# Two input loads, a pair of first maxima and the last batches' small work at other places in a cross-attention kernel

## The chip, the core and the metric

The kernel runs on one core of a Trainium2 chip. The core has five engines with queues of their own: TensorE (PE in the profile; its weight loads are listed apart as PEld), VectorE (DVE), ScalarE (ACT), GpSimd (POOL) and SyncE (SP). Each engine works through its queue in order, and SP does nothing here but issue DMA transfers. POOL issues a few transfers too, on a DMA queue of its own. The metric is device time in microseconds of one execution, the median over several runs; lower is better. Beside it there is one profiled execution, from which all rows of the profile come.

## The reference

Eight batches of 112 queries with 320 channels attend to 375 context rows of 512 channels. The last four context rows are image prompts (IP), the other 371 are text. There are 20 heads of 16 channels. In short:

```python
q   = heads(x @ W_q);  k_t = heads(text @ W_k);  v_t = heads(text @ W_v)
probs_t  = softmax(q k_t^T / 4)                     # 112 x 371 for each batch and head
text_out = probs_t @ v_t
qsem  = l2norm(probs_t @ text)                      # 112 x 512 for each head
sem   = qsem @ l2norm(ip)^T                         # 112 x 4
fused = q k_ip^T / 4 + 0.5 * sem
ip_out = (softmax(fused) * mask) @ v_ip
out = (text_out + ip_out) @ W_out + b_out + x
```

The kernel does not form `qsem`. It multiplies the probabilities by a matrix with the context's Gram matrix, the products with the prompts and the head's values side by side; the norm follows from the Gram part by a product with the probabilities and a sum, `ss`.

## The kernel before

The work of a batch is cut into five groups of four heads, so there are 40 steps (b, g). For one step:

- TensorE makes four scores, one for each head (`scores`, L648).
- VectorE takes the first maxima of their rows, negated (`probabilities`, L661, tile `nmx`). ScalarE does the exps with them (L665, tile `p`) and for later batches copies the four prompt logits (L667, `ipl`).
- SP copies the four probabilities into another arrangement (L672, `xg` from `p`; `xg` is one of a ring of two tiles), and VectorE transposes 32x32 blocks of it (`transposed`, L684, `xgT`). A step's transposes can be done in two halves.
- TensorE does the products with `u`, the Gram matrix and the values: 12 blocks of rows of four heads each (`product`, L696, into `ps_qd`).
- VectorE multiplies the Gram part with the probabilities and sums (`reduced`, L749), and ScalarE copies the value part (`value_sums`, L723, tile `pvs`). For the last batch some heads go another way: `shared(b, g, n)` gives n of a group's four heads to ScalarE (copies L733 and L734, sums L742) and POOL (products L738), and `reduced` does the rest.
- POOL puts the values into `u` for the next steps (`placed`, L614).

`finish(b)` is what remains for a batch: a generator that yields between its pieces. It normalises, does the small softmax over the prompts, multiplies with the prompts' values on POOL (L831, L834), adds both halves to the attention `ah` (L838, L839), transposes it on TensorE (L844, `ps_a`), projects it (L853, `ps_o`), adds input and bias (L859, `ob`) and writes it out. `run(key, make, pieces)` advances a generator by that many pieces. The last batch (b = 7) has `ending` in place of it; in its case the input and the bias are added by `with_bias(b)` (L763) on POOL. `x_sb` holds the inputs; `load_inputs(b0, b1)` (L308) loads those of some batches with one transfer of POOL's queue.

The order on each engine is written by hand: the scope is `manual_schedule`, and instructions stand in each queue in the order of the program. After a start, `alone(0)` does the products of the first step. From then on `pair(n)` does two steps, n and n + 1, in one stream of products, with the scores, maxima and exps of the steps two ahead placed among the products, and `behind(n)` does what lies between pairs: keys, values, queries and Gram matrices of the next batches, and pieces of `finish`. `steps` has its index n from 0, so pair(1) is (0,1) and (0,2), pair(3) is (0,3) and (0,4), pair(5) is (1,0) and (1,1), pair(7) is (1,2) and (1,3). A loop over the last batch's groups closes the program, with the pieces of batch 6's `finish` (key `before`) between its steps.

In `pair(n)`, `coming_scores` and `coming_probabilities` are called for the heads (2, 3) at j = 0 and for (0, 1) at j = 1, and the second half of the next step's transposes follows at j = 1. The first half is done by the `tr(1)` of the `behind` before. The transfers of SP use eight semaphores in turn, so that a transfer waits until the one eight before it has landed.

Of the kernel before, what the change touches and what calls it, by code (L numbers as in the profile page):

```python
# [20 lines left out]
def kernel(  # L21
# [588 lines left out]
    def placed(b, g, chunks=range(NT)):  # L610

        s = st[b]
        for c in chunks:
            nc.gpsimd.tensor_copy(  # L614
                region(b, c)[:, :, UV - c * P :], s["vr"][:, c * QN : (c + 1) * QN, g, :]
            )
# [149 lines left out]
    def finish(b):  # L766
# [65 lines left out]
            if some.stop < NIP:  # L832
                yield
        eng.tensor_tensor(wv[:, :2], wv[:, :2], wv[:, 2:], ALU.add)  # L834
        if b == B - 2:
            yield
            eng = nc.vector
        eng.tensor_tensor(ah, ah, wv[:, 0], ALU.add)  # L838
        eng.tensor_tensor(ah, ah, wv[:, 1], ALU.add)  # L839
        yield  # L840

        ps = bank(f"ps_a_{b}", spare=True)
# [246 lines left out]
    def alone(n):  # L1089
# [5 lines left out]
                    coming_probabilities(n + LEAD, heads)  # L1095
        transposed(*steps[n + 1])

    def pair(n):

        one, two = steps[n], steps[n + 1]  # L1100
        b, g = one
        tags = ("mm", "sc") if b % 2 and g == NG - 1 else ("sc", "mm")
        ends = (BLK - 2, BLK - 1)

        products_in(b, g, ("qd",) * GROUP)
        for j in range(BLK - 2):
            product(b, g, j, range(GROUP))
            if j < 2:
                heads = (HIGH, LOW)[j]
                coming_scores(n + LEAD, heads, tags[j])  # L1110
                coming_probabilities(n + LEAD, heads)
            if j == 1:
                transposed(*two, BLK // 2, BLK)
            if j % QN == QN - 1:
                placed(*two, (j // QN,))
        products_in(*two, (tags[1],) * 2 + (tags[0],) * 2)
        for there, here in ((HIGH, LOW), (LOW, HIGH)):
            product(*two, 0, there)
            for j in ends:
                product(b, g, j, here)  # L1120
        del st[b]["xT", g]
        placed(*two, (NT - 1,))
        moved(b, g)
        if g > 1:
            turned(b + 2)
        if b % 2 and g in (0, NG - 1):
            f(b - 1 - (g == 0))
        if g in (1, 2):
            f(b - 1, 3 - g)
        reduced(b, g)  # L1130
        value_sums(b, g)

        b, g = two
        for j in range(1, BLK - 2):
            product(b, g, j, range(GROUP))
            if j == 4:
                coming_scores(n + 1 + LEAD, HIGH, "qd")
                coming_probabilities(n + 1 + LEAD, HIGH)
            if j == 7:
                coming_scores(n + 1 + LEAD, LOW, "qd")  # L1140
                coming_probabilities(n + 1 + LEAD, LOW)
        for heads in (HIGH, LOW):
            for j in ends:
                product(b, g, j, heads)
        del st[b]["xT", g]
        moved(b, g)
        if one in ((b, 2), (b, 3)):
            turned(b + 2, 1 + (one == (0, 3)))
# [17 lines left out]
    def behind(n):  # L1166
# [9 lines left out]
        if b % 2 == 0 and g == 0:  # L1176
# [15 lines left out]
            v(nb)  # L1192
            if n == 0:
                run(("pp",), prompt_projections)
            tr(1)
            if n:
                f(b - 1, 2)
            load_next(b + 2)
            if n == 0:
                load_inputs(1, 3)  # L1200
        elif b % 2 == 0 and g == 2:
            turn[:] = ["qd"] * (6 + (b == 0)) + ["mm"]
            gram_to_groups(nb, (2,))
            if b == 0:
                run(("pp",), None)
            k(nb)
            q(nb, 3)
            tr(0)
            v(nb)
            q(nb)  # L1210
            v(nb)
            if b == 0:
                run(("pp",), None)
            tr(1)
            values_to_dram(nb, nc.sync)
            if b == 0:
                load_channels(nc.gpsimd, wo_sb, w_out)
                nc.gpsimd.dma_start(sm_sb, smask.unsqueeze(1))
                nc.gpsimd.dma_start(bias_sb, b_out.partition_broadcast(S))
            elif b == 2:  # L1220
                load_inputs(5, B)
        elif b % 2 == 0 and nb < B - 1:
            if b == 0:
                load_inputs(3, 5)
            turn[:] = ["qd"] * (4 + (b > 0)) + ["mm", "mm"]
            turned(b + 2)
            q(nb)
            if b > 0:
                f(b - 1)
            else:  # L1230
                run(("t", b), lambda: prompt_logits(b))
            k(nb)
            tr(0)
            if b > 0:
                f(b - 1)
            gr(nb + 1, 3)
            tr(1)
            if b > 0:
                f(b - 1)
            load_next(b + 3)  # L1240
            f(b)
            prompt_values(b)
        elif b % 2 == 0:
            turn[:] = ["qd"] * 4 + ["mm"]
            q(nb, 2)
            f(b - 1)
            k(nb)
            nc.scalar.preload_act_table(AF.Sqrt)
            tr(0)
            f(b - 1, 2)  # L1250
            prompt_values(b)
            f(b, 2)
        elif g == 1:
            turn[:] = ["qd"] * 4 + ["mm"]
            gram_to_groups(nb, (2,))
            q(b)
            k(b)
            nc.scalar.preload_act_table(AF.Sqrt)
            k(nb)
            tr(0)  # L1260
            f(b - 1)
            v(nb)
            tr(1)
            v(nb)
            f(b - 1, 3)
            values_to_dram(nb, nc.sync, 0, 2)
            if b == B - 3:
                prompt_values_by_head()
        else:
            turn[:] = ["qd"] * 3 + ["sc"]  # L1270
            v(nb)
            f(b - 1)
            values_to_dram(nb, nc.sync, 2)
            tr(0)
            k(nb)
            f(b - 1, 2)
            tr(1)
            gram_to_groups(nb, (3,))
            values_to_groups(nb, 2)
# [41 lines left out]
    for g in range(NG):  # L1321
        if g == 1:
            run(("f", b - 2), None)
        for j, _ in enumerate(multiplied(b, g)):
# [7 lines left out]
            if g == 1 and j == BLK // 2:  # L1332
                last_keys(b, ps_qd.tile([P, 512], F32, tag="qd", name=f"ps_k_{b}_{FULL}"))
                run(before, None)
                placed(b, g + 1, (0,))
                with_bias(b)
            if g == 2 and j == 2:
                transposed(b, g + 1)
            if g == 3 and j == 3:
                placed(b, g + 1, (0,))  # L1340
                run(before, None)
                transposed(b, g + 1)
                drain(sums)
        if g == NG - 1:
            break

        n = (3, 3, 2, 1)[g]
        held, sums = sums, shared(b, g, n)
        value_sums(b, g, n)
        next(sums)  # L1350
# [2 lines left out]
        reduced(b, g, n)  # L1353
        placed(b, g + 1, range(g % 2, NT))
        if g > 1:
            run(before, None)
        drain(held)
        next(sums)
    run(before, None)
    drain(sums)  # L1360
    last = ending(b, bd)
    next(last)
    reduced(b, g, 0, 1)
    value_sums(b, g, 1)
    run(before, None)
    next(last)
    value_sums(b, g, 0, 1)
    reduced(b, g, 1)
    next(last)
    run(before, None)  # L1370
    next(last)
    next(last)
    next(last)
    run(before, None, 2)
# [45 lines left out]
```

## Time and profile before

| | us |
|---|---|
| median of 3 runs | 419.34 (417.5 to 419.59) |
| profiled execution | 421.68 |
| its span, first to last instruction | 419.9 |
| mean granted clock of TensorE in it | 0.995 of full speed |
| TensorE busy | 410.9 |
| VectorE busy | 326.9 |
| ScalarE busy | 188.6 |
| POOL busy | 113.2 |

A row of the timeline gives the start and the length in microseconds, the engine, the line, the operation, the tile written and the tile read, and the number of instructions that the row joins; in brackets stands the idle time of that engine before it and what ended it. SPq is the issue of transfers by SP; an issue's length is not the transfer's. A window's row gives, for each engine, busy time and number of instructions, then the granted clock, the share of the 16 DMA engines and the rate.

### The profile page before, as it was taken

The page shows a single profiled execution, that of the slowest core. Times are in us where ns is not written, and L with a number is a line of the kernel's source. Part 1 is how long each engine was busy: PE and PEld are TensorE (multiplying, and loading weights), DVE is VectorE, ACT ScalarE, POOL GpSimd, SP SyncE. Part 2 cuts the span into 40 slices and gives each one's busy share as a digit, 9 for nine tenths or more (in the row PEclk, how much of TensorE's full clock was granted, in tenths as well). Part 3 has the DMA queues.
Part 4 walks back from the last instruction along what each step waited for, and adds up shares of the span by engine and source line. Part 5 has one row for each costly group of instructions (what it writes and reads, how often), then busy time and mean ns, then how long its engine had stood idle before and what let it go on. Part 6 is the DMA issues. An engine that isn't in the chain of part 4 may idle for free.

```text
span 419.9 us, 14045 instructions
## 1 busy us (share of the span) xinstructions
PE 410.9 (98%) x5609; PEld 323.1 (77%) x5609; DVE 326.9 (78%) x694; ACT 188.6 (45%) x655; POOL 113.2 (27%) x265
## 2 busy tenths in 40 slices
PE   8999999989999999999999999999999999999896
PEld 8867788868687877879686877779877878687894
DVE  4256686956889888786889897787888987888985
ACT  3254342333642734423643554333644365346853
POOL 4203130031160244011242136002025126104670
PEclk9999999998999999999999999999999999999999
DMA  8878967686555667676655476567756344666220
GB/s 237 170 187 245 168 157 172 168 213 153 129 145 138 169 144 176 168 171 156 165 139 135 123 171 162 149 165 164 176 143 166 100 120 123 173 151 188 85 65 27
DMA packets 58244, 64.64 MB, mean 154 GB/s; under 512 B 19061, under 2 KB 52041, under 8 KB 58180
## 3 DMA queue, kind: packets, MB, share of 16 engines
q1 hardware_dynamic: 57150, 61.47, 58.3%
q0 software_dynamic: 464, 1.56, 1.7%
q8 instruction: 44, 0.72, 0.8%
q10 hardware_dynamic: 566, 0.72, 0.5%
q14 instruction: 20, 0.16, 0.1%
HBM read 19.03 MB, written 5.22 MB: 58 GB/s over the span
## 4 chain that ended last, share of the span: by engine, by line
PE 91%; SPq 2%; DVE 2%; ACT 1%; POOL 1%; DMA 1%; issue 1%; POOLq 0%
PE ps_qd L696 43%; PE ps_v L533 13%; PE ps_k L494 9%; PE ps_g L468 7%; PE ps_s L648 6%; PE ps_q L339 3%; PE ps_k L511 3%; PE ps_o L853 2%; PE ps_g L438 1%; PE ps_w L425 1%; DMA vr<-vd 1%; SPq L482 1%; SPq L136 1%; PE ps_c L408 1%; PE ps_x L331 0%
## 5 line engine op out<-in xcount | busy, mean ns | idle before, releaser
L696 PE MATMUL ps_qd<-u,xgT 32*112 32x40 f32 (+11 forms) x3840 | 220.0, 354 | 3.4 <-ACT ipl L667 1.8
L696 PEld LDWEIGHTS ps_qd<-u,xgT 32*112 32x112 f32 x3840 | 182.5, 173 | 38.1 <-issue 8.7
L684 DVE STREAM_TRANSPOSE xgT<-xg 128x768 f32<-128x768 f32 (+1 forms) x63 | 123.4, 1977 | 17.3 <-DMA xg<-p 9.5
L665 ACT ACTIVATE p<-ps_s,nmx 112x371 f32<-112x371 f32 x160 | 85.5, 585 | 66.9 <-DVE nmx L661 66.7
L661 DVE TENSOR_REDUCE nmx<-ps_s 112x1 f32<-112x371 f32 x160 | 77.1, 535 | 32.2 <-PE ps_s L648 30.0
L614 POOL COPY u<-vr 128x64 f32<-128x64 f32 x120 | 26.8, 236 | 216.7 <-PE ps_qd L696 133.3
L749 DVE CUSTOM_DVE_ANT_0 p<-ps_qd,p 112x371 f32<-112x371 f32 x151 | 72.8, 538 | 11.4 <-ACT pvs L723 8.3
L648 PE MATMUL ps_s<-kT,qm 32*112 32x375 f32 (+1 forms) x320 | 60.9, 485 | 0.0
L533 PE MATMUL ps_v<-wv_sb,ctxT 128*128 128x320 f32 x192 | 56.1, 439 | 0.3 <-ACT kT L501 0.3
L533 PEld LDWEIGHTS ps_v<-wv_sb,ctxT 128*128 128x128 f32 x192 | 35.3, 190 | 14.7 <-ACT kT L501 1.2
L723 ACT COPY pvs<-ps_qd 112x21 f32<-112x21 f32 x151 | 21.6, 197 | 53.0 <-DVE ss L749 48.2
L494 PE MATMUL ps_k<-ctxT,wk_sb 128*128 128x371 f32 x128 | 43.6, 484 | 0.0
L494 PEld LDWEIGHTS ps_k<-ctxT,wk_sb 128*128 128x128 f32 x128 | 23.0, 190 | 13.2 <-issue 1.3
L468 PE MATMUL ps_g<-ctxT 128*32 128x119 f32 (+11 forms) x672 | 33.0, 343 | 0.0
L468 PEld LDWEIGHTS ps_g<-ctxT 128*32 128x32 f32 x672 | 26.2, 109 | 7.4 <-issue 4.2
L648 PEld LDWEIGHTS ps_s<-kT,qm 32*112 32x112 f32 x320 | 28.0, 171 | 4.8 <-ACT p L665 0.4
L396 DVE STREAM_TRANSPOSE ctxT<-ct 128x512 f32<-128x512 f32 x21 | 22.3, 1072 | 6.9 <-DMA u<-ug 6.9
L540 ACT COPY vext<-ps_v 128x320 f32<-128x320 f32 x24 | 10.2, 425 | 36.3 <-PE ps_v L533 33.9
L667 ACT COPY ipl<-ps_s 112x4 f32<-112x4 f32 x140 | 24.2, 173 | 0.0
L454 ACT ACTIVATE ug<-ps_g 128x375 f32<-128x375 f32 (+2 forms) x24 | 9.1, 377 | 23.3 <-PE ps_g L468 9.0
L455 POOL TENSOR_TENSOR ug<-ug,half 128x128 f32<-128x128 f32 (+1 forms) x24 | 10.6, 451 | 29.2 <-ACT ug L454 29.2
L501 ACT COPY kT<-ps_k 128x371 f32<-128x371 f32 x16 | 7.5, 469 | 22.8 <-PE ps_k L494 22.5
(150 smaller groups left out, 318.9 us busy)
## 6 DMA issues: line engine op xcount, KB each, us to landing
xg<-p SPq DMA_DIRECT2D x159, 162.3 KB
u<-ug SPq DMA_DIRECT2D x128, 99.0 KB
ct<-in_ctx_dram SPq DMA_DIRECT2D x28, 176.0 KB
vip<-vipd SPq DMA_DIRECT2D x7, 560.0 KB
vr<-vd SPq DMA_DIRECT2D x20, 120.0 KB
vd<-vext SPq DMA_DIRECT2D x14, 160.0 KB
vd<-vext SPq DMA_DIRECT2D x28, 40.0 KB
out_dram<-ob SPq DMA_DIRECT2D x7, 140.0 KB
```

The source lines that it names most:

```text
L396: nc.vector.transpose(ctxT[:, :, c * P : (c + 1) * P].rearrange("p e (j i) -> p j e i", i=RG), ct[:, some, :].rearrange("p j (k e) -> p j ...
L468: nc.tensor.matmul(ps[p * RG : (p + 1) * RG, s0 : T - t0], ctxT[:, e, t0 + q * RG : t0 + (q + 1) * RG], ctxT[:, e, t0 + s0 : T], start=(e ...
L494: nc.tensor.matmul(ps[:, :TT], wk_sb[:, e, i * P : (i + 1) * P], s["ctxT"][:, e, :TT], start=(e == 0), stop=(e == NE - 1),)
L533: nc.tensor.matmul(ps[:, :C], ctxT[:, e, c * P : (c + 1) * P], wv_sb[:, e, :], start=(e == 0), stop=(e == NE - 1),)
L614: nc.gpsimd.tensor_copy(region(b, c)[:, :, UV - c * P :], s["vr"][:, c * QN : (c + 1) * QN, g, :])
L648: nc.tensor.matmul(ps[:S, :w], qm[a * RG : (a + 1) * RG, i, r, j * S : (j + 1) * S], s["kT"][a * RG : (a + 1) * RG, i, :w], start=True, st ...
L661: nc.vector.tensor_reduce(nmx, ps[:S, :TT], AX.X, ALU.max, negate=True)
L665: nc.scalar.activation(p, ps[:S, :TT], AF.Exp, bias=nmx)
L667: nc.scalar.copy(s["ipl"][:, groups[g][a], :], ps[:S, TT:T])
L684: nc.vector.transpose(xT[:, j : j + n].rearrange("p j (k q) -> p q j k", q=QN), xg[:, :, j * RG : (j + n) * RG].rearrange("p q (j k) -> p ...
L696: nc.tensor.matmul(banks[a][:S, j * RG : UW], xT[a * RG : (a + 1) * RG, j, :S], region(b, c)[a * RG : (a + 1) * RG, p, q * RG :], start=(j ...
L749: nc.vector.tensor_tensor_reduce(out=p, in0=ps[:S, :TT], in1=p, scale=1.0, scalar=0.0, op0=ALU.mult, op1=ALU.add, accum_out=s["ss"][:, h : ...
```

## The change

There are three parts. The diff below has all of them.

1. In pair(1), the first half of the transposes of (0,2), which `behind(0)` placed ahead of the pair, is now placed at j = 1, just ahead of the second half. So on VectorE the four maxima of (0,3) stand ahead of this half and no longer behind it.
2. `load_inputs(3, 5)` moves from `behind(4)`, ahead of pair(5), to pair(1); `load_inputs(5, 8)` moves from `behind(12)` to pair(7). Both are placed after the first ten blocks of products of the pair's first step.
3. At the end: the bias addition of the last batch comes one step later (group 2 instead of group 1), behind the products of `shared` in POOL's queue. `shared` takes no head of group 3 (one before), so VectorE does four reductions there instead of three. The two additions of batch 6 are now done by POOL instead of VectorE, in two pieces; on POOL the first stands ahead of the division of the last batch, the second behind it. Batch 6's transposes on TensorE stand behind the last batch's first ones and the transposes of `bd`, and its `ob` on VectorE comes ahead of the last batch's `sx`, `rx` and `w`, not behind them.

SP's order is the same in both kernels. TensorE's differs only at the end, by the transposes of batch 6.

```diff
--- before.py
+++ after.py
@@ -832,11 +832,10 @@
             if some.stop < NIP:
                 yield
         eng.tensor_tensor(wv[:, :2], wv[:, :2], wv[:, 2:], ALU.add)
-        if b == B - 2:
-            yield
-            eng = nc.vector
-        eng.tensor_tensor(ah, ah, wv[:, 0], ALU.add)
-        eng.tensor_tensor(ah, ah, wv[:, 1], ALU.add)
+        for i in range(2):
+            if b == B - 2:
+                yield
+            eng.tensor_tensor(ah, ah, wv[:, i], ALU.add)
         yield
 
         ps = bank(f"ps_a_{b}", spare=True)
@@ -1095,6 +1094,8 @@
                     coming_probabilities(n + LEAD, heads)
         transposed(*steps[n + 1])
 
+    inputs = {1: (3, 5), 7: (5, B)}
+
     def pair(n):
 
         one, two = steps[n], steps[n + 1]
@@ -1110,9 +1111,13 @@
                 coming_scores(n + LEAD, heads, tags[j])
                 coming_probabilities(n + LEAD, heads)
             if j == 1:
+                if n == 1:
+                    transposed(*two, 0, BLK // 2)
                 transposed(*two, BLK // 2, BLK)
             if j % QN == QN - 1:
                 placed(*two, (j // QN,))
+        if n in inputs:
+            load_inputs(*inputs[n])
         products_in(*two, (tags[1],) * 2 + (tags[0],) * 2)
         for there, here in ((HIGH, LOW), (LOW, HIGH)):
             product(*two, 0, there)
@@ -1192,8 +1197,8 @@
             v(nb)
             if n == 0:
                 run(("pp",), prompt_projections)
-            tr(1)
             if n:
+                tr(1)
                 f(b - 1, 2)
             load_next(b + 2)
             if n == 0:
@@ -1217,11 +1222,7 @@
                 load_channels(nc.gpsimd, wo_sb, w_out)
                 nc.gpsimd.dma_start(sm_sb, smask.unsqueeze(1))
                 nc.gpsimd.dma_start(bias_sb, b_out.partition_broadcast(S))
-            elif b == 2:
-                load_inputs(5, B)
         elif b % 2 == 0 and nb < B - 1:
-            if b == 0:
-                load_inputs(3, 5)
             turn[:] = ["qd"] * (4 + (b > 0)) + ["mm", "mm"]
             turned(b + 2)
             q(nb)
@@ -1333,9 +1334,9 @@
                 last_keys(b, ps_qd.tile([P, 512], F32, tag="qd", name=f"ps_k_{b}_{FULL}"))
                 run(before, None)
                 placed(b, g + 1, (0,))
-                with_bias(b)
             if g == 2 and j == 2:
                 transposed(b, g + 1)
+                with_bias(b)
             if g == 3 and j == 3:
                 placed(b, g + 1, (0,))
                 run(before, None)
@@ -1344,7 +1345,7 @@
         if g == NG - 1:
             break
 
-        n = (3, 3, 2, 1)[g]
+        n = (3, 3, 2, 0)[g]
         held, sums = sums, shared(b, g, n)
         value_sums(b, g, n)
         next(sums)
@@ -1353,22 +1354,20 @@
         reduced(b, g, n)
         placed(b, g + 1, range(g % 2, NT))
         if g > 1:
-            run(before, None)
+            run(before, None, g - 1)
         drain(held)
         next(sums)
-    run(before, None)
     drain(sums)
     last = ending(b, bd)
     next(last)
+    run(before, None)
     reduced(b, g, 0, 1)
     value_sums(b, g, 1)
-    run(before, None)
     next(last)
     value_sums(b, g, 0, 1)
     reduced(b, g, 1)
     next(last)
-    run(before, None)
-    next(last)
+    run(before, None, 2)
     next(last)
     next(last)
     run(before, None, 2)
```

## The prediction

> **What bounds the kernel now.** I read the page first: busy shares, then the chain that ended last.
>
> ```profile
> span 419.9 us, 14045 instructions
> PE 410.9 (98%) x5609; PEld 323.1 (77%) x5609; DVE 326.9 (78%) x694; ACT 188.6 (45%) x655; POOL 113.2 (27%) x265
> PE 91%; SPq 2%; DVE 2%; ACT 1%; POOL 1%; DMA 1%; issue 1%; POOLq 0%
> ```
>
> TensorE is the bound nearly everywhere. An edit on another engine can pay only where TensorE is held up or its matmuls stretch, so I looked for such places. A pair is the same work each time, so I took from the timeline of TensorE the row that opens a pair and the row that opens the next stage, for the second, fourth and sixth step, which the code calls pair(1), pair(3) and pair(5).
>
> ```profile
> 45.54 1.22 PE L696 MATMUL ps_qd<-u,xgT 32*112 32x392 f32 x10
> 57.20 0.35 PE L289 MATMUL ps_kipT<-ident,kv 32*128 32x32 f32 x3
> 66.43 0.93 PE L696 MATMUL ps_qd<-u,xgT 32*112 32x392 f32 x8
> 77.17 1.02 PE L339 MATMUL ps_q<-xT,wq_sb 128*128 128x224 f32 x4
> 86.23 1.22 PE L696 MATMUL ps_qd<-u,xgT 32*112 32x392 f32 x10
> 101.72 1.02 PE L339 MATMUL ps_q<-xT,wq_sb 128*128 128x224 f32 x4
> ```
>
> The stretches last 11.66, 10.74 and 15.49 us. Against pair(3), pair(1) loses 0.92 and pair(5) 4.75. Those 5.67 us are most of what this change can reach. First pair(1), from the timeline of all engines:
>
> ```profile
> 47.01 1.17 SPq L141 DMA_DIRECT2D ct<-in_ctx_dram  x3
> 47.20 0.48 PE L648 MATMUL ps_s<-kT,qm 32*112 32x371 f32 x2
> 48.06 1.57 DVE L684 STREAM_TRANSPOSE xgT<-xg 128x768 f32<-128x768 f32 x1 [3.23 <-DMA xg<-p]
> 49.48 1.82 DVE L661 TENSOR_REDUCE nmx<-ps_s 112x1 f32<-112x371 f32 x4
> 50.59 4.01 SPq L672 DMA_DIRECT2D xg<-p  x4
> 52.00 2.34 PEld L696 LDWEIGHTS ps_qd<-u,xgT 32*112 32x112 f32 x42 [0.19 <-ACT p L665]
> ```
>
> The four scores of (0,3) are done at 47.68. Their maxima stand on VectorE behind a transpose that waits for a transfer until 48.06, and start at 49.48. The exps follow, then SP's copies, and TensorE's weight loads end a wait on exps at 52.00. Now pair(5), with the window of 95 to 99 us, in which the number behind the counts of POOL is the granted clock:
>
> ```profile
> 82.33 3.66 SPq L672 DMA_DIRECT2D xg<-p  x4
> 90.16 1.57 DVE L684 STREAM_TRANSPOSE xgT<-xg 128x768 f32<-128x768 f32 x1 [5.02 <-DMA ct<-in_ctx_dram]
> 91.88 1.89 DVE L661 TENSOR_REDUCE nmx<-ps_s 112x1 f32<-112x371 f32 x4
> 93.17 6.09 PE L696 MATMUL ps_qd<-u,xgT 32*112 32x392 f32 x57 [1.84 <-ACT ipl L667]
> 95.00:99.00 4.00, 4.00 (x46) 3.02 (x42) 2.01 (x9) 0.71 (x4) 0.24 (x1) 0.57 0.65 170
> ```
>
> The same order of transpose and maxima, with a transfer that comes later. The transpose starts 3.93 us after the pair opens (90.16 against 86.23); in pair(1) it was 2.52. The releaser is named as a context load, but that was issued only from 86.03 on; I read it as the copies xg of (1,1), whose last issue ends at 85.99. TensorE idles 1.84 us, then runs four microseconds at a mean clock of 0.57: another 1.7 us.
>
> **Part one: the maxima move ahead of the transpose in pair(1).** Nothing is added: one transpose changes places with four maxima on VectorE. They can follow the scores, so begin between 46.8 and 47.7 instead of 49.48. Then both transposes end near 52.0, before the second step of the pair needs them. TensorE loses nothing there: 0.9 us gained; bounds 0 (if TensorE waits there for something else, a rival below) and 0.92. What is late next is the transpose of the second half, which VectorE still does last of the three and no later than today.
>
> **Part one, seen from SP.** The first copy left 1.1 us after the maxima began (50.59 against 49.48). It can leave at 48.2, where SP is done with its context loads (47.01 + 1.17), if its ring place is free. So SP's queue starts up to 2.4 us earlier; at least 0.9, because TensorE is that much ahead. From 50.59 to 85.99 SP issued 44 transfers, the first four and the last four in rows above; by the same timeline they take 34.75 of 35.40 us, so a lead at the start is still there at the end. I take 2.
>
> **What that makes of pair(5).** I need what xg's copies take from the end of their issue to the transpose that waits, and what start costs nothing. The rows are from the timelines of VectorE, SP and POOL, the DMA view of 88 to 90 us, and the view of the loads' line:
>
> ```profile
> 67.64 1.57 DVE L684 STREAM_TRANSPOSE xgT<-xg 128x768 f32<-128x768 f32 x1 [2.44 <-DMA u<-ug]
> 181.08 3.65 SPq L672 DMA_DIRECT2D xg<-p  x4
> 187.42 1.66 DVE L684 STREAM_TRANSPOSE xgT<-xg 128x768 f32<-128x768 f32 x1 [1.15 <-DMA xg<-p]
> 58.43 3.63 SPq L672 DMA_DIRECT2D xg<-p  x4
> 59.12 0.74 POOL L119 DMA_DIRECT2D wo_sb<-in_L_xattn_W_out_dram  x1
> 60.94 0.54 POOL L1219 DMA_DIRECT2D bias_sb<-in_L_xattn_b_out_dram  x1
> q0 software_dynamic: 74, 0.27, 54.4%
> L309 POOL DMA_DIRECT2D x_sb<-in_x_dram x3: 712/756/847, 46.6 to 161.5; - x3
> DMA to landing us min/median/max: 5.5/6.0/6.3
> ```
>
> Undisturbed it is 2.69 us (184.73 to 187.42); for (1,1) it was 4.17; for (0,4), with four loads of POOL's queue beside it (the first and the last are shown), 5.58 (62.06 to 67.64). In pair(3) a start 1.21 us in cost nothing. After the change the pair opens at 85.31, and issue ends at 84.0. By 2.69 us the transpose starts at 86.7, 1.4 in: between 1.21 (nothing) and 2.52 (0.92) that is 0.1 lost. By 4.17 us it starts 2.9 in, and between 2.52 (0.92) and 3.93 (4.75) that is some 1.9 lost. With a lead of only 0.9 and 4.17 us nothing changes: 4.75.
>
> **Part two: the load of x_sb(3,5) leaves this stage.** Beside (1,1) ran the load of POOL's queue: POOL's queue q0 took 54.4% of the 16 engines from 88 to 90 us. It goes to pair(1). So the landing is nearer 2.69 than 4.17; I take 0.35 lost, a gain of 4.4 with bounds 0 and 4.75. The Trainium skill, in DMA: Bandwidth & Descriptors (Queues, rings and completion order), says that each DMA engine takes its queues in turn, a packet at a time; the q0 share here agrees, and the same rule would have the load hold up whatever it is moved beside. On POOL its issue is 0.71 to 0.85 us, between u's copies:
>
> ```profile
> 53.13 0.24 POOL L614 COPY u<-vr 128x64 f32<-128x64 f32 x1 [2.53 <-PE ps_qd L696]
> 117.83 0.24 POOL L614 COPY u<-vr 128x64 f32<-128x64 f32 x1 [1.30 <-PE ps_qd L696]
> 397.72 0.24 POOL L614 COPY u<-vr 128x64 f32<-128x64 f32 x1 [0.97 <-PE ps_qd L696]
> 114.23 3.67 SPq L672 DMA_DIRECT2D xg<-p  x4
> 125.26 2.98 DVE L684 STREAM_TRANSPOSE xgT<-xg 128x1536 f32<-128x1536 f32 x1
> ```
>
> Idle 2.53 hides it. x_sb(5,8) likewise goes before the copy at 117.83, idle 1.30, and the bias of the last batch, an addition of 0.86 like L838 below, before the one at 397.72, idle 0.97. Each costs nothing; without its cover a copy would be late by the operation, under 0.9. The transfers land some 6 us after issue. x_sb(3,5), issued near 51, is in by 57, beside the copies xg(0,3): if these took 5.58 instead of 2.69 us, they would land near 58, and the pair that multiplies them opens at 66.43, 65.5 then. x_sb(5,8) runs beside xg(1,4), whose issue ends at 117.90: at 5.58 it lands at 123.5, and its transpose starts at 125.26. Both are hidden.
>
> **Part three: the end.**
>
> ```profile
> 408.16 1.25 DVE L838 TENSOR_TENSOR attn<-attn,wv 112x320 f32<-112x320 f32 x1 [0.40 <-POOL wv L834]
> 409.44 0.49 DVE L839 TENSOR_TENSOR attn<-attn,wv 112x320 f32<-112x320 f32 x1
> 410.18 0.63 POOL L890 TENSOR_TENSOR attn<-pvs,zr 112x256 f32<-112x256 f32 x1 [1.12 <-DVE zr L889]
> L838 POOL TENSOR_TENSOR attn<-attn,wv x6: 858/864/867, 122.2 to 355.1; 112x320 f32<-112x320 f32 x6
> 411.32 1.27 PE L853 MATMUL ps_o<-wo_sb,aT 128*112 128x320 f32 x4
> ```
>
> VectorE sheds two additions (1.74) and takes a reduction more, whose copy, product and sum leave ScalarE and POOL. POOL is done with L834 when the first of them starts (408.16), then does an addition (0.86) to 409.0, the division (0.63) to 409.7 instead of 410.81, and the second addition to 410.6 instead of 409.93 on VectorE. So the last batch's transposes come some 0.7 to 1 us earlier, and batch 6's products (411.32) 0.3 to 0.5 later; they then stand in front of the last batch's remaining products. Between -0.5 and +0.5; I take +0.1, since the later part is nearer the end.
>
> **Sum:** -0.9 - 4.4 + 0.1 = -5.2. The profiled execution took 421.68 (span 419.9 and 1.78 around it): 416.5. It is 2.34 above the median of 419.34, so the other runs may have lost less in pair(5). Subtracting everything gives 414.1; without the half clock's 1.7, 415.8. I lean to the first: **414.3**.
>
> **Rivals.** *Only pair(1) gains.* The copies of (1,1) come late whatever SP does, so pair(5) keeps its loss: 419.34 - 0.9 + 0.1 = 418.5. For it: the lead of 2 is not seen anywhere yet. Against: SP's back-to-back issues.
>
> *The clock still falls.* The stall goes, but the half clock, 1.7 us, turns up elsewhere: 416.0. For it: it fell after 95 us, some two microseconds after TensorE's wait was over. Against: no second such stretch in the profile. The Trainium skill, in TensorE: Matmul & The Clock Gate (Part 1), ties half rate to an idle free-running window of about 3.4 us; here 1.84 us of idling was enough, so the trace does not agree in size, though by that rule this stall should not have cost a clock at all, which is this rival.
>
> *The order does nothing.* If TensorE in pair(1) waits for u's copies rather than exps, and pair(5) stays: 419.4.
>
> *Slower.* The moved x_sb(3,5) takes DMA engines beside xg(0,3), and the ring places of SP's later transfers free up late: SP loses its lead and more. POOL's loads cost (0,4) 2.9 us (5.58 against 2.69). To end above 421.4, pair(5) must lose 3.0 more than now, so SP must be 2.1 later than now, a swing of some 4: at 4.1, 421.5; at 5, 422.4. Against it: the load is one, where four cost 2.9.
>
> **How the numbers follow.** Chances: forecast 0.60, clock 0.10, only pair(1) 0.14, nothing 0.08, slower 0.08. About 0.5% (2.1 us) is what a measurement can tell from no change: under 417.2 is faster (0.60 + 0.10 + a little of pair(1) = 0.72), the rest of two cases the same (0.20). The forecast's own range is 413.0 to 416.0; reaching 8 in 10 needs the clock case and the pair(1) case, so 412.8 to 418.7.
>
> **What would show it.** Right: maxima ahead of the half transpose near 47 and SP's copies before 49; a pair(1) of 10.8; a pair(5) whose transpose starts within 1.5 us and no clock of 0.5 behind it; no q0 at that place. Wrong: SP's xg(1,1) still issued after 81.5 relative to a pair that opens at 85.3, an idle TensorE before a first half, a stall after 117 or 52 behind POOL's new load, or a wait of the last batch's products on batch 6's at 412.

## The result: 0.9 per cent faster, and where the profile shows it

| | before | after |
|---|---|---|
| median, us (22 runs each) | 420.97 (417.5 to 424.75) | 417.29 (414.74 to 420.67) |
| ratio after to before | | 0.9913, 95% interval 0.9887 to 0.9939 |
| profiled execution, us | 421.68 | 419.46 |
| its span, us | 419.9 | 417.7 |
| mean granted clock in it | 0.995 | 0.998 |

The change makes the kernel 3.7 us faster, with an interval of 2.6 to 4.8 (the ratio's ends on 420.97). Both kernels vary by 6 to 7 us from run to run. The 22 runs of before have a higher median than the three that were shown (420.97 against 419.34). Here and below a ratio leaves out runs that took over 1.5 per cent more than the fastest of their kernel, and it is not exactly the quotient of the medians. Neither profile is a typical execution: the one after is 2.2 us above its kernel's median, the one before 0.7, so the two profiles together show less than the change gives over the runs. The profile after, its totals, and the rows of TensorE that open pair(1), pair(3), pair(5) and the stages behind them:

```profile
span 417.7 us, 14048 instructions
PE 408.8 (98%) x5609; PEld 318.9 (76%) x5609; DVE 324.7 (78%) x694; ACT 188.1 (45%) x652; POOL 114.1 (27%) x266
```

```profile
45.50 1.22 PE L696 MATMUL ps_qd<-u,xgT 32*112 32x392 f32 x10
56.39 0.35 PE L289 MATMUL ps_kipT<-ident,kv 32*128 32x32 f32 x3
65.63 1.22 PE L696 MATMUL ps_qd<-u,xgT 32*112 32x392 f32 x10
78.55 1.21 PE L339 MATMUL ps_q<-xT,wq_sb 128*128 128x224 f32 x5
87.62 1.22 PE L696 MATMUL ps_qd<-u,xgT 32*112 32x392 f32 x10
100.33 1.40 PE L339 MATMUL ps_q<-xT,wq_sb 128*128 128x224 f32 x6
```

The pairs last 10.89, 12.92 and 12.71 us; before they lasted 11.66, 10.74 and 15.49. So pair(1) gains 0.77, pair(3) loses 2.2 and pair(5) gains 2.8: of the 2.2 us by which this profiled execution is shorter, 1.4 come from these three. Comparing the start of the same matmul in both traces, the only other stage ahead of the last batch that differs by more than 0.1 us is that from 183 to 200 us (17.83 before, 17.07 after). It lasted between 17.07 and 18.0 in the profiles of the experiments too, without order, so it is not put down to the change.

pair(1) is as forecast. From the timeline after:

```profile
47.09 1.95 DVE L661 TENSOR_REDUCE nmx<-ps_s 112x1 f32<-112x371 f32 x4 [2.31 <-PE ps_s L648]
48.58 4.31 SPq L672 DMA_DIRECT2D xg<-p  x4
48.95 2.95 DVE L684 STREAM_TRANSPOSE xgT<-xg 128x768 f32<-128x768 f32 x2
```

The maxima start at 47.09 instead of 49.48 and wait for scores only, SP's copies leave at 48.58 instead of 50.59, and both transposes end at 51.90. pair(3) is where a new wait stands:

```profile
56.77 5.01 SPq L672 DMA_DIRECT2D xg<-p  x4
61.83 7.64 SPq L482 DMA_DIRECT2D u<-ug  x8
69.03 1.57 DVE L684 STREAM_TRANSPOSE xgT<-xg 128x768 f32<-128x768 f32 x1 [4.46 <-DMA u<-ug]
71.68 4.31 PE L696 MATMUL ps_qd<-u,xgT 32*112 32x392 f32 x55 [0.96 <-ACT ipl L667]
```

Before, four copies of (0,4) took SP 3.63 us and the eight transfers behind them 5.97; now 5.01 and 7.64. What SP waited for is told by the view of its own waits (us in total, times, longest), from 56.5 to 70 us after:

```profile
SPq L482 <- DMA xg<-p: 2.8, 2, 2.5
SPq L672 <- DMA xg<-p: 1.5, 2, 0.9
```

and from 58.4 to 68.2 us before:

```profile
SPq L482 <- DMA xg<-p: 1.1, 2, 0.6
```

So the issues of xg(0,4) (L672) now wait 1.5 us for copies xg(0,3) to land, which they did not before, and those of u (L482) 2.8 us for copies xg(0,4). The lead of 2.0 us that SP had at 48.58 has become a delay: pair(3)'s transpose starts 3.40 us after its opening (1.21 before), and TensorE waits. In pair(5):

```profile
83.37 3.66 SPq L672 DMA_DIRECT2D xg<-p  x4
90.44 1.57 DVE L684 STREAM_TRANSPOSE xgT<-xg 128x768 f32<-128x768 f32 x1 [3.97 <-DMA xg<-p]
93.46 4.40 PE L696 MATMUL ps_qd<-u,xgT 32*112 32x392 f32 x57 [0.75 <-POOL u L614]
95.00:99.00 4.00, 4.00 (x72) 3.61 (x74) 2.91 (x11) 0.73 (x5) 0.47 (x2) 1.00 0.60 161
```

The copies of (1,1) leave 1.0 us later than before in absolute time, 4.25 us ahead of the opening instead of 3.90. The transpose starts 2.82 us in instead of 3.93. TensorE idles 0.75 us where it idled 1.84, and the clock stays at 1.00 (0.57 before).

### The profile page after: what moved, and what is told of

Read it like the earlier page. It is cut to its first block, busy times and chain, and to the rows that moved or that the text cites. A ratio compares the mean times of both kernels' runs of the same rounds, so it can differ in the third digit from the quotient of the medians.

```text
span 417.7 us, 14048 instructions
## 1 busy us (share of the span) xinstructions
PE 408.8 (98%) x5609; PEld 318.9 (76%) x5609; DVE 324.7 (78%) x694; ACT 188.1 (45%) x652; POOL 114.1 (27%) x266
## 4 chain that ended last, share of the span: by engine, by line
PE 88%; DMA 6%; ACT 2%; DVE 2%; issue 1%; POOL 0%; SPq 0%; DVEq 0%; POOLq 0%
PE ps_qd L696 40%; PE ps_v L533 12%; PE ps_k L494 9%; PE ps_g L468 8%; DMA xg<-p 6%; PE ps_s L648 6%; PE ps_q L339 3%; PE ps_o L852 3%; PE ps_k L511 2%; DVE xgT L684 1%; PE ps_g L438 1%; ACT p L665 1%; PE ps_w L425 1%; PE ps_c L408 1%; DVE nmx L661 0%
## 5 line engine op out<-in xcount | busy, mean ns | idle before, releaser
L696 PEld LDWEIGHTS ps_qd<-u,xgT 32*112 32x112 f32 x3840 | 178.7, 172 | 39.7 <-issue 7.1
L684 DVE STREAM_TRANSPOSE xgT<-xg 128x768 f32<-128x768 f32 (+1 forms) x63 | 123.1, 1974 | 16.6 <-DMA xg<-p 10.9
```

What stands on the lines that cost most here:

```text
L684: nc.vector.transpose(xT[:, j : j + n].rearrange("p j (k q) -> p q j k", q=QN), xg[:, :, j * RG : (j + n) * RG].rearrange("p q (j k) -> p ...
L696: nc.tensor.matmul(banks[a][:S, j * RG : UW], xT[a * RG : (a + 1) * RG, j, :S], region(b, c)[a * RG : (a + 1) * RG, p, q * RG :], start=(j ...
```

## The experiments

Each kernel was timed in the same session as before, and its ratio is to that. All pair lengths and offsets below are worked out like those above, from the row that opens a pair, the row that opens the next stage and the first transpose.

**One part at a time.** The transpose alone:

```diff
             if j == 1:
+                if n == 1:
+                    transposed(*two, 0, BLK // 2)
                 transposed(*two, BLK // 2, BLK)
...
-            tr(1)
             if n:
+                tr(1)
                 f(b - 1, 2)
```

> Only the half transpose moves behind the maxima in pair(1); both loads and the end stay as before. Theory A (SP's lead carries to pair(5); the moved load was what ate it in the changed kernel): pair(1) 0.8 shorter, pair(3) as before, the transpose of pair(5) starts within 2 us of its opening, so some 3 us less there; the time falls by 3.5 to 5 us. Theory B (the load of x_sb(3,5) beside xg(1,1) makes the stall of pair(5)): only pair(1) gains, 0.8 us, pair(5) still lasts over 14.5 us.

Measured: 417.44 us against 420.81, ratio 0.9895 (0.9852 to 0.9938). pair(1) lasts 10.92, pair(3) 10.70, pair(5) 11.59. Rows of pair(5), with x_sb(3,5) still loaded beside it:

```profile
81.57 3.66 SPq L672 DMA_DIRECT2D xg<-p  x4
86.49 1.22 PE L696 MATMUL ps_qd<-u,xgT 32*112 32x392 f32 x10
88.20 1.56 DVE L684 STREAM_TRANSPOSE xgT<-xg 128x768 f32<-128x768 f32 x1 [2.77 <-DMA xg<-p]
93.00:97.00 4.00, 4.00 (x77) 3.61 (x76) 2.90 (x11) 0.97 (x5) 0.47 (x2) 1.00 0.98 192
```

SP is 4.92 us ahead of the opening and the transpose starts 1.71 us in. Theory A holds: this part alone gives as much as the whole change, within the intervals.

The load of x_sb(3,5) alone, moved from its old place into pair(1):

```diff
+        if n == 1:
+            load_inputs(3, 5)
         products_in(*two, (tags[1],) * 2 + (tags[0],) * 2)
...
-            if b == 0:
-                load_inputs(3, 5)
```

> Only x_sb(3,5) moves to pair(1). Theory A: xg(0,3) and xg(0,4) land late, pair(3) loses 1.5 to 3 us, pair(5) gains at most 1 or keeps its loss; time 0 to 2.5 us longer than before. Theory B: pair(5) loses its stall, the time falls by 2 to 4 us, with pair(3) losing less than 1.

Measured: 419.19 against 420.81, ratio 0.9936 (0.9904 to 0.9969). Theory A had it slower, and it is not. Theory B's numbers came out: by the ratio 2.7 us are gained, pair(3) lasts 10.70 and pair(5) 11.28. The same load taken away from pair(5) but put into pair(7), where it is beside nothing that is late:

```diff
+    inputs = {7: (3, 5)}
...
+        if n in inputs:
+            load_inputs(*inputs[n])
         products_in(*two, (tags[1],) * 2 + (tags[0],) * 2)
...
-            if b == 0:
-                load_inputs(3, 5)
```

> Before with x_sb(3,5) in pair(7) and nothing else. pair(1) 11.7 as before. Theory A (SP's lead matters, the load does not): pair(5) 14.5 or more with the half clock, time within 1 us of before. Theory B (the load beside xg(1,1) makes the stall): pair(5) 11 to 12.5, no half clock, 3 to 4 us below before. That both reliefs are enough each by itself is what the first four runs suggest; then B's numbers here.

Measured: 420.02 against 420.25, ratio 0.9961 (0.9923 to 1.0000). Rows of its pair(5):

```profile
82.91 3.66 SPq L672 DMA_DIRECT2D xg<-p  x4
86.52 1.22 PE L696 MATMUL ps_qd<-u,xgT 32*112 32x392 f32 x10
90.25 1.56 DVE L684 STREAM_TRANSPOSE xgT<-xg 128x768 f32<-128x768 f32 x1 [4.82 <-DMA xg<-p]
95.00:99.00 4.00, 4.00 (x43) 3.06 (x42) 2.17 (x9) 0.71 (x4) 0.24 (x1) 0.57 0.67 183
```

In this profile the stall and the half clock stand without the load: pair(5) lasts 15.31. It is one execution, the longest of twelve (421.15). The time is against theory B as the main cause too, since 3 to 4 us were expected of it and the ratio gives 1.6; but the interval reaches from 0 to 3.2 us, so that the load's leaving pair(5) is worth something is not excluded. Why its move into pair(1) gained in the run before this one is not shown. In the profile of that run TensorE came to pair(5) 1.2 us later than before, mostly because of waits near 20 to 45 us that differ between executions, while SP's copies of (1,1) left 0.4 later, so its lead there was 4.74.

The end alone:

```diff
...
-        n = (3, 3, 2, 1)[g]
+        n = (3, 3, 2, 0)[g]
```

(with the bias, the additions and the pieces of `finish` as in the change; transposes and loads as before)

> Only the edits at the end. By the comparison of the two profiles: 1.2 us gained ahead of the third group of the last batch, where the copies of u no longer stand behind the bias addition, some 1.1 given back where the fifth group waits for its xg, and the last ten us as long as before: within 0.5 us of before, pieces as named. Rival: the gain is not given back (the giving back came from an earlier TensorE in the changed kernel): 1 us shorter.

Measured: 422.32 against 420.81, ratio 1.0021 (0.9989 to 1.0053): no difference. TensorE's waits in the last batch, of before and then of this kernel:

```profile
394.05 1.70 PE L696 MATMUL ps_qd<-u,xgT 32*112 32x392 f32 x14 [1.10 <-ACT shared L734]
405.18 1.23 PE L696 MATMUL ps_qd<-u,xgT 32*112 32x392 f32 x12 [0.33 <-ACT pvs L733]
```

```profile
403.71 2.96 DVE L684 STREAM_TRANSPOSE xgT<-xg 128x768 f32<-128x768 f32 x2 [1.19 <-DMA xg<-p]
405.40 0.93 PE L696 MATMUL ps_qd<-u,xgT 32*112 32x392 f32 x8 [1.25 <-DVE xgT L684]
```

The wait of 1.10 ahead of the third group is gone, and one of 1.25 stands ahead of the fifth, whose transfer does not come earlier. In the changed kernel the same: 1.40 there. The reason that was expected for the gain is not what the traces show. POOL's copy of u starts 0.66 us after the row of products that ends the second group before (392.29 against 391.63), and 0.65 us after it with the end alone (392.63 against 391.98), and waits for TensorE both times. What differs is an operation of VectorE beside the bias addition. Before, and then with the end alone:

```profile
389.96 1.63 DVE L809 TENSOR_TENSOR fu<-pvs,rn 112x80 f32<-112x80 f32 x1
390.63 0.86 POOL L763 TENSOR_TENSOR bd<-x_sb,bias_sb 112x320 f32<-112x320 f32 x1
```

```profile
390.30 0.24 DVE L809 TENSOR_TENSOR fu<-pvs,rn 112x80 f32<-112x80 f32 x1
```

Before, L809 ends 0.10 us after POOL's addition does, and behind it on VectorE stand the transposes that the third group's products need. They start 2.12 us after the keys' products (L511, 390.23) before and 0.96 after them (390.58) with the end alone, a difference of 1.16. ScalarE's copies, which the row above names, start equally late in both, 1.85 and 1.86 us after those products. It is so in all profiles: in the eight whose bias addition stands at its old place L809 or the operation behind it, L810, takes 1.52 to 1.63 us, and in the five in which it comes later L809 takes 0.24 and L810 0.47 to 0.49.

**The moved load in pair(1).** Does it make the 2.2 us of pair(3)? First the change without the part at the end, so the kernel with the transposes moved and both loads as in the change:

```diff
+    inputs = {1: (3, 5), 7: (5, B)}
...
+        if n in inputs:
+            load_inputs(*inputs[n])
         products_in(*two, (tags[1],) * 2 + (tags[0],) * 2)
...
-            if b == 0:
-                load_inputs(3, 5)
```

> The changed kernel with the end as before: transposes moved and both loads moved. Theory A (x_sb(3,5) in pair(1), beside an xg(0,3) that now leaves earlier, holds up the ring of SP's transfers): pair(3) lasts 12 to 13.5 us as in the changed kernel, and the time is 1 us or more longer than with the transposes alone, so 2.5 to 3.5 below before. Rival: the 2.2 us in pair(3) were one execution's; pair(3) lasts 10.7 and the time is 4 to 5 us below before.

Measured: 416.71 against 420.25, ratio 0.9921 (0.9881 to 0.9961). pair(3) lasts 10.70 and pair(5) 10.70; SP's four copies of (0,4) take 3.93. So in this execution the load did not hold SP up, though its edits are those of the changed kernel. The pair lengths are the rival's, the median, 3.5 below before, is theory A's. The transfers themselves differed between the two executions. The load of x_sb(3,5), with its size and its time from issue to landing, in the changed kernel and then here:

```profile
x_sb<-in_x_dram POOLq DMA_DIRECT2D x1, 280.0 KB, 8.5
```

```profile
x_sb<-in_x_dram POOLq DMA_DIRECT2D x1, 280.0 KB, 5.6
```

The load of 280 KB before it, issued at 46.6 us in both, took 7.1 and 5.4 us. Why transfers are slower in one execution is not shown. Then the dose: one load of x_sb(3,8), two and a half times as large, at that place, and none later.

```diff
-    inputs = {1: (3, 5), 7: (5, B)}
+    inputs = {1: (3, B)}
```

> Transposes moved, the end as before, and one load of x_sb(3,8) in pair(1), two and a half times what the change loads there; no load later. Theory A (a load beside xg(0,3) holds SP's ring): the issue of xg(0,4) waits and lasts over 4.5 us, pair(3) lasts 12 to 14 us or pair(5) over 12.5, and the time is only 0 to 2.5 us below before. Rival (the 2.2 us of pair(3) in the changed kernel were one execution's chance, the load has room): 3.5 us or more below before.

Measured: 419.39 against 419.66, ratio 0.9990 (0.9952 to 1.0028). The gain is gone.

```profile
56.15 5.03 SPq L672 DMA_DIRECT2D xg<-p  x4
61.23 9.40 SPq L482 DMA_DIRECT2D u<-ug  x8
65.91 1.22 PE L696 MATMUL ps_qd<-u,xgT 32*112 32x392 f32 x10
70.18 1.55 DVE L684 STREAM_TRANSPOSE xgT<-xg 128x768 f32<-128x768 f32 x1 [5.51 <-DMA xg<-p]
72.83 5.90 PE L696 MATMUL ps_qd<-u,xgT 32*112 32x392 f32 x56 [1.82 <-ACT ipl L667]
74.00:78.00 4.00, 4.00 (x37) 3.29 (x39) 3.57 (x10) 1.00 (x6) 0.23 (x1) 0.57 0.48 144
```

SP's rows are those of the changed kernel, larger: 5.03 and 9.40. pair(3)'s transpose starts 4.27 us in, pair(3) lasts 15.31, and the half clock is now here. pair(5) lasts 10.70, since TensorE came late and SP not. So a load beside xg(0,3) does hold up SP's queue and through it pair(3). With the change's own size pair(3) was held up in one profile of three (12.92; 10.70 in two, one with the transposes moved and one without), and in that one the load ahead of it was slow too, so the moved load's own share in its 2.2 us is not shown.

**The loads out of the way of both.** The changed kernel with the loads in pair(7) and pair(17), first with the change's end and then with the end as before:

```diff
-    inputs = {1: (3, 5), 7: (5, B)}
+    inputs = {7: (3, 5), 17: (5, B)}
```

> The changed kernel with x_sb(3,5) loaded in pair(7) and x_sb(5,8) in pair(17). Theory A: pair(3) loses nothing, pair(5) little; 2 to 4 us faster than the changed kernel, 5 to 8 us faster than before. Theory B: the same as the changed kernel within 1 us.

Measured: 417.24 against 420.81, ratio 0.9891 (0.9847 to 0.9934); pairs 10.89, 10.70, 12.90.

> Transposes moved, x_sb(3,5) in pair(7), x_sb(5,8) in pair(17), the end as before. pair(1) 10.9, pair(3) 10.7, pair(5) 11 to 13 with no half clock: 4 to 5.5 us below before. If the end's edits are worth something, it is slower than the kernel of the run with late loads by up to 0.5; if they cost, faster by as much.

Measured: 416.52 against 420.25, ratio 0.9892 (0.9845 to 0.9939); pairs 10.89, 10.70, 12.69. The two ends make no difference. pair(3) loses nothing, as theory A says, but pair(5) kept 2 us of its stall in both, so the 5 to 8 us expected of the first did not come, and neither kernel is shown to be faster than the changed one. The 4 to 5.5 us expected of the second came out by the ratio (4.5).

**The wait ahead of the fifth group.** In the changed kernel, the exps of the last group start 0.6 us after their first maximum, behind three sums of the first group on ScalarE:

```diff
-                with_bias(b)
             if g == 2 and j == 2:
                 transposed(b, g + 1)
+                with_bias(b)
+                drain(held)
...
-        drain(held)
+        if g != 1:
+            drain(held)
```

on the kernel with late loads and the end as before.

> The kernel with late loads and the end as before, and two pieces of the last batch placed later: its bias addition as in the change, and the sums of its first group on ScalarE behind the exps of its last group. In the changed kernel the 1.1 us gained ahead of the third group were lost before the fifth, whose exps started 0.6 us after their first maximum, behind three sums. Theory: the exps start at once, xg(7,4) comes 0.5 to 0.6 earlier, so 0.6 to 1.0 us faster than with late loads alone. Rival: the transfer itself took longer, the wait stays and nothing is gained (within 0.3).

Measured: 415.01 against 420.25, ratio 0.9880 (0.9826 to 0.9935). From before the third group to the fifth its profile has 16.08 us (4.25 and 11.83), where the kernel without this edit has 17.15 (5.27 and 11.88): 1.1 us gained, of which the fifth group's products give back a quarter (4.98 against 4.73). The exps now start at once, but TensorE's wait ahead of the fifth group is still 0.96 us (1.07 without the edit); by the profile it now ends with POOL's copies of u. The gain stands ahead of the third group, where the bias is gone. The whole is the lowest ratio of all, but the intervals overlap with the changed kernel's and with that of late loads alone, so the expected 0.6 to 1.0 us are not shown by the time.

**SP's lead by another way.** Four loads of POOL's queue (the output weights in two parts, mask and bias) ran beside xg(0,4). They are moved from near 59 us to pair(5), first alone and then on top of the last kernel:

```diff
+        if n == 5:
+            load_channels(nc.gpsimd, wo_sb, w_out)
+            nc.gpsimd.dma_start(sm_sb, smask.unsqueeze(1))
+            nc.gpsimd.dma_start(bias_sb, b_out.partition_broadcast(S))
...
-            if b == 0:
-                load_channels(nc.gpsimd, wo_sb, w_out)
-                nc.gpsimd.dma_start(sm_sb, smask.unsqueeze(1))
-                nc.gpsimd.dma_start(bias_sb, b_out.partition_broadcast(S))
```

> Before with only those four loads moved to pair(5); transposes, x_sb and the end as before. Theory A (SP's lead makes pair(5)): pair(1) 11.7 as before, the lead of xg(1,1) on the opening of pair(5) grows from some 3.7 to 4.7 us or more, pair(5) falls to 11 to 12.5 without a half clock, time 2 to 4 us below before. Theory C (only an earlier VectorE in pair(1) gives the lead): pair(5) 14.5 or more, within 1 us of before.

Measured: 419.69 against 419.66, ratio 1.0009 (0.9977 to 1.0041).

```profile
81.99 3.66 SPq L672 DMA_DIRECT2D xg<-p  x4
86.99 1.22 PE L696 MATMUL ps_qd<-u,xgT 32*112 32x392 f32 x10
90.30 1.57 DVE L684 STREAM_TRANSPOSE xgT<-xg 128x768 f32<-128x768 f32 x1 [4.39 <-DMA xg<-p]
```

The lead grew to 5.00 as theory A says, but the copies took 4.65 us from the end of their issue to the transpose, beside x_sb(3,5), which is still there; pair(5) lasts 13.20. The time is not below before's, against theory A's 2 to 4: pair(5) is 2.3 us shorter in this profile, but over the runs nothing is gained, and why stays open.

> The kernel with late loads and bias and sums later, and the four loads of wo_sb, the mask and the bias moved from behind(2) (near 59 us) to pair(5) (near 97 us). Theory A: xg(0,4) lands 2 to 3 us after its issue, SP's ring is free, and xg(1,1) leaves 1 to 2 us earlier against the opening of pair(5); pair(5) 10.7, the time 0.5 to 2 us below that kernel without this edit, 5.5 to 7 below before, and less spread. Rival: pair(5) is no longer bound there, no change within 0.5.

Measured: 415.69 against 419.66, ratio 0.9895 (0.9861 to 0.9930), with a spread of 414.42 to 416.45 over nine runs. xg(1,1) leaves 6.63 us ahead and pair(5) lasts 10.70, but the kernel without this edit had 6.57 and 10.70 in its profile too. No further gain is shown.

**All profiles together.** Each row is one execution. For pair(5): how far ahead of its opening the first copy of (1,1) leaves, what lies between the end of the issue and the first transpose, how far in that transpose starts, the length, and the clock behind it.

| kernel | lead | issue end to start | start | length | half clock |
|---|---|---|---|---|---|
| before | 3.90 | 4.17 | 3.93 | 15.49 | yes |
| end alone | 3.70 | 3.96 | 3.92 | 15.00 | yes |
| x_sb(3,5) in pair(7) alone | 3.61 | 3.68 | 3.73 | 15.31 | yes |
| four loads to pair(5) alone | 5.00 | 4.65 | 3.31 | 13.20 | no |
| changed, loads late | 4.06 | 3.40 | 3.00 | 12.90 | no |
| changed | 4.25 | 3.41 | 2.82 | 12.71 | no |
| transposes and late loads | 4.36 | 3.51 | 2.81 | 12.69 | no |
| transposes alone | 4.92 | 2.97 | 1.71 | 11.59 | no |
| x_sb(3,5) in pair(1) alone | 4.74 | 2.46 | 1.38 | 11.28 | no |
| transposes and both loads | 5.53 | 2.49 | 0.62 | 10.70 | no |
| transposes, x_sb(3,8) in pair(1) | 6.20 | 2.56 | 0.02 | 10.70 | no |
| late loads, bias and sums later | 6.57 | 2.56 | -0.35 | 10.70 | no |
| the same, four loads to pair(5) | 6.63 | 2.48 | -0.49 | 10.70 | no |

Above a start of about 0.8 us each microsecond costs one (1.38 gives 0.58 lost, 3.31 gives 2.50), and between 3.31 and 3.73 another 1.7 comes in with the clock. Only the end alone lies 0.5 below that line.

**How often the half clock comes.** The granted clock of each execution is on record, rounded to three digits. The four profiles with a half clock in a pair have a mean of 0.995 or 0.996, the nine others 0.998 or more, and no execution lies between. By that mark 36 of the 71 executions of before in the three sessions have such a stretch, 5 of 22 of the changed kernel, and none of 27 of four kernels with the transposes moved (transposes alone, the first two with late loads, the last one with the four loads moved). With the end alone it is 11 of 12. With x_sb(3,5) put into pair(7) it is 3 of 12, and the profile above is one of the three; with the larger load it is 3 of 12 too, and 1 or 2 in each of the four others. So a pair(5) of 15.49 us is not the rule in before: about every second execution has it, if the half clock stands in pair(5) there as it does in the profiles.

## Why the prediction was right, point by point

**The time.** Forecast 414.3, or 0.988 of the median then shown, and measured 0.9913. The sign, the stage and the order of size were right; the gain was 3.7 us instead of 5. That 417.29 lies between 412.8 and 418.7 owes something to luck: it is above the forecast's own range (413.0 to 416.0), and inside the stated one only because that was widened for two rivals, neither of which came true as described; and the three runs behind 419.34 were 1.6 below the median of 22. In the two profiles pair(1), pair(3), pair(5) and the end add up to -0.8 + 2.2 - 2.8 + 0.1 = -1.3 us, against the forecast's -5.2, and the loss in pair(3) is a term that the sum did not have.

**pair(1), -0.9.** Right: -0.77, with the maxima near 47 and SP's copies before 49 as named. All eight profiles with this edit have 10.9, all others 11.7 to 12.4.

**SP's lead of 2 is still there at the end of its 44 issues.** Half right. The lead was there at 48.58, and 2.0 against before is 1.2 against a TensorE that is 0.8 ahead. The 34.75 us of 35.40 were not issue alone, since a row's length holds the waits between its issues: the eight of u take 5.02 to 9.40 us in these profiles. So the argument from back-to-back issues holds only while no transfer waits longer for the one eight before it to land, and in the changed kernel's profile those waits took the lead: relative to pair(5)'s opening the lead was 0.35 us larger than before, and 1.0 in the run of the transposes alone.

**The load of x_sb(3,5) is hidden beside xg(0,3).** This is the step that failed. It was priced by when xg(0,3) itself is needed, near 65.5, and not by who waits for xg(0,3) to land on SP: the issues of xg(0,4), one round of eight behind. The profile after lost 2.2 us in pair(3) by this way, in an execution with slow transfers, and the larger load 4.6, of which 1.7 by the half clock; in two other profiles the change's load was hidden as forecast. The rival called slower had the mechanism, but looked for it in pair(5), where a swing of 4 us was needed; in pair(3), one stage earlier, SP's 2 us of lead were enough to lose.

**The load's leaving pair(5) brings the landing nearer 2.69 than 4.17.** Not shown: it was 3.41 in the changed kernel, and between 2.46 and 3.68 in profiles without the load there; with it 2.97 to 4.65. Taking it away alone did not shorten pair(5) in the one profile of that kernel. The Trainium skill's rule in DMA: Bandwidth & Descriptors (Queues, rings and completion order) is that each DMA engine takes its queues in turn. What the prediction had follow from it, that a load holds up what it is moved beside, the dose bears out in pair(1) (the gain of 1.05% became 0.10%); for pair(5) it is not shown.

**pair(5), -4.4.** Measured -2.8 in the profile. The term was sized by a line from 1.21 (nothing) over 2.52 (0.92) to 3.93 (4.75), whose first two points belong to pair(3) and pair(1); the points of the table give 0.8 for pair(5)'s free start and a slope of one, so even the start of 1.4 that was forecast costs 0.6, not 0.1. The rival called slower reckoned with a slope of one, so the two sums did not agree with each other. The 4.75 also had the half clock in it, which only about every second execution of before has.

**The end, +0.1.** Right in sum, by parts that were not seen. From the keys' products ahead of the third group (L511) to the transpose of the last batch's weights (L973, L972 after) the profile has 25.15 us, 25.07 before. The bias, said to cost and gain nothing, gained 1.1 us ahead of the third group, where it no longer runs beside VectorE's work on the small softmax, and about as much was given back ahead of the fifth, in the changed kernel and with the end alone. Between the two kernels with late loads, which differ in the end only, 1.0 us is gained and 0.2 given back, and still their times do not differ.

**Which rivals fell.** Only pair(1) gains: no, the transposes alone gave 4.4 by the ratio (1.05% of 420.81). The order does nothing: no. The clock still falls: not in the profile after, but in 5 of 22 executions by the mean clock. Slower: no, though its mechanism showed in pair(3).

## What to carry to other kernels

When an in-order DMA queue limits transfers in flight, a load put beside one transfer is paid by the issue that waits for that transfer's place, a round later; price it there, not at the consumer. A small stall may cost more than itself where the clock follows, so take the step that shortens the longest wait first: here one transpose moved behind four maxima gave by itself about what the whole change gave. A change that removes one wait close to the end needs the next wait looked up, since an off-path transfer may be the bound right behind it. And one profile shows one execution: before sizing a term by a stall, see from the times and clocks on record how many executions have it.

## What was not expected of the hardware

In the profiles the half clock came each time TensorE idled 1.66 us or more in a pair (1.84 before and with the end alone, 1.66 with x_sb(3,5) in pair(7), 1.82 with the larger load in pair(1)), and never at 1.24 or less (1.24 with the four loads moved, 0.75 and 0.96 in the changed kernel). The two rows on either side, TensorE in pair(5) with x_sb(3,5) in pair(7) and then with the four loads moved:

```profile
93.26 3.50 PE L696 MATMUL ps_qd<-u,xgT 32*112 32x392 f32 x31 [1.66 <-ACT ipl L667]
```

```profile
93.32 3.06 PE L696 MATMUL ps_qd<-u,xgT 32*112 32x392 f32 x36 [1.24 <-ACT ipl L667]
```

But the length of the idle time is not shown to be what decides; its place may be. By the trace the half clock of before lasts from 95.30 to 98.71 us, 3.41 us, and does not start with the idle time (91.33 to 93.17) nor with its end. The stretch itself, the one of equal length ahead of it and the one behind it:

```profile
95.30:98.71 3.41, 3.41 (x30) 2.44 (x28) 1.71 (x8) 0.71 (x4) 0.24 (x1) 0.50 0.60 157
91.90:95.29 3.39, 2.12 (x28) 1.61 (x32) 3.39 (x7) 2.19 (x8) 0.00 (x0) 1.00 0.76 214
98.72:102.00 3.28, 3.28 (x73) 3.21 (x66) 1.99 (x4) 1.62 (x6) 0.54 (x3) 1.00 0.57 130
```

In all four profiles with it the half clock lasts 3.41 us, and from the first full clock of the trace to its start there are 88.75 us (68.27 with the larger load), which is 26 (20) times 3.413. So the clock looks to be set in fixed stretches of 3.41 us. In the stretch just ahead of the half clock TensorE was busy for 62, 46, 56 and 47 per cent by the profile. With the four loads moved such a boundary falls at 92.75, inside the idle time of 1.24 us, which is so split over two stretches, busy for 80 and 83 per cent. Outside the pairs an idle time of 1.52 us, ahead of the fifth group in the profile of x_sb(3,5) in pair(1) alone, is split likewise and has no half clock behind it. But near the end of the program stretches busy for 59 per cent (the end alone) and 63 per cent (changed, loads late) have none either, and no run here moves an idle time against these boundaries, so what share of a stretch must be idle stays open.

The Trainium skill, in TensorE: Matmul & The Clock Gate (Part 1), names an idle window of about 3.4 us. The length of the stretch agrees with it here; that the window be idle does not, since TensorE was busy for about half of it.

The other thing is VectorE beside POOL: L809, an operation of 0.24 us, took 1.63 us beside POOL's bias addition. In the kernel with late loads and the end as before L810 stood beside the addition, and took 1.52 us instead of 0.47 to 0.49:

```profile
386.42 1.52 DVE L810 SCALAR_TENSOR_TENSOR fu<-fu,ipl 112x80 f32<-112x80 f32 x1
```

So the addition, which POOL did in idle time, cost VectorE over a microsecond, and through the transposes behind it TensorE as much.
